# The weights of a spectral mix in halves through the ring of x, and loads moved across a stage boundary

## The chip, the cores and the metric

The kernel runs on one core of a Trainium2 chip. The metric is the device time of one execution in microseconds (us). Three timed runs of the kernel before gave a median of 3059.18 us (3055.52 to 3066.23). The profile is of one further execution, which took 3042.76 us; its span, from the first instruction to the last, is 3041.0 us.

The engines are PE (matrix products; PEld is its weight load), DVE and ACT (element-wise work; both can read PE's result memory, PSUM), POOL (element-wise work without PSUM, and DMAs), and SP (DMAs only). DMAs are issued on three queues, those of SP, ACT and POOL, and run on the same 16 DMA engines. Every queue, like every engine, takes its instructions in program order.

## The reference

The input x is (8, 32, 256, 256): 8 images, 32 channels, 256 x 256. Four layers follow each other; each normalises x over groups of two channels (zero mean, unit variance), applies a convolution of some kind and adds the result to x. The change lies in the first layer and in its seam with the second.

```
out_lo = einsum('bixy,ioxy->boxy', rfft2(gn(x))[:, :, :32, :32], w1)      # layer 0: 32 x 32 low modes,
out_hi = einsum('bixy,ioxy->boxy', rfft2(gn(x))[:, :, -32:, :32], w2)     # complex weights per mode
x = x + irfft2(zeros with out_lo, out_hi in their places) + bias
x = x + conv5x5(gn(x))                                                    # layer 1: one 5 x 5 kernel for all
x = x + gru_over_columns(gn(x))                                           # layer 2: recurrence along w
x = x + W @ [x, four running maxima of x] + b                             # layer 3
```

## The kernel before

**Forward transform and mix** (`forward_and_mix`). The forward transform goes over 64 units (`units`, eight images b by eight groups n of four channels). A unit's x is one tile `xa` of 1 MB (8 KB in each of 128 partitions), loaded by SP (L116) into a ring of AHEAD = 7 buffers: six loads are issued ahead, and then, ahead of unit u's work, that of unit u + 6. `over_columns(u)` (L118) multiplies by the constants `fw` (32 matmul records), squares x on ACT and on DVE (L140, L141) for the variance, and turns the result on DVE (L144) into `y`; its PSUM tile `yp` has three buffers. `over_rows(b, i)` (L148), four slices for an image, uses the constants `fh` and stands, for image b - 1, between the units 0 to 3 of image b. `turn`, `statistics` and `normalise` of image b - 1 come at the units 4, 5 and 7; `normalise` (L198) scales on DVE (L201), writes one half of the spectrum `xf` on ACT (L202) and the other, with real and imaginary parts swapped, by four POOL DMAs (L206).

The order is written out by hand (`manual_schedule(engines=None)`): each engine gets its instructions as the program lists them.

The mix (L252 on) has eight sets q of four kx; a set takes 256 recorded matmuls of 64 x 64 by 32, 128 for each half of ky. The weights of a set, `wt`, are 2 MB. Set 0 has a pool of its own, `mw`, and is loaded at unit (7, 2) (L217); sets 1 to 7 use a pool `mw2` of five buffers (L247) that is opened after the forward transform's pools are closed, so that its first loads wait for these. Results are copied from PSUM by ACT and DVE into `sm` (two buffers for each of two signs) and stored to the DRAM scratch `smd` on ACT's and SP's queue (L287).

**Inverse transform and 5 x 5 convolution** (`inverse_and_conv`). It goes over 16 units of 16 channels. `load_spectrum(b)` (L348) reads image b's spectrum from `smd` in three DMAs: one of 64 rows of 8 KB (L351) and two that pick 128 bytes at a time (L353), for images 0 and 1 on SP, later on ACT. `load(u, i)` (L383) reads a third of a unit's x, `xb`, in two POOL DMAs of 768 KB. Ahead of the loop stand the spectra of images 0 and 1, the x of unit 0, the sign turn of a half of spectrum 0 on DVE (L358), then `spectrum` (L369), a chain of small DVE instructions on the mean, and the inverse transform's matmuls (L410, L427).

**Around them.** `load_consts` (L39) issues eleven small loads on SP, and L107 that of `fh` (1 MB), ahead of x. `recurrence_weights` (L687) loads 384 KB `weights` and two small biases on POOL's queue and adds the biases on DVE (L698, L699), which waits for both; it is called ahead of everything else (L1089). `recurrence` and `maxima_and_mix`, some 2,000 us of the span, are not touched.

Of the kernel before, what the change touches and what calls it, by code (L numbers as in the profile page):

```python
# [9 lines left out]
F32 = mybir.dt.float32  # L10
# [6 lines left out]
P = 128  # L17
B, C, H, W = 8, 32, 256, 256
NG = 16
KM = 32  # L20
# [4 lines left out]
Q = H // A  # L25
# [13 lines left out]
def load_consts(tc, pool, d):  # L39
    nc = tc.nc  # L40
    k = Consts()
    for name in ("sign", "sel", "msel", "fw", "gw", "eh", "ident", "ident32", "pair", "valid", "conv"):
        t = pool.tile(list(d[name].shape), F32, name=f"c_{name}")
        nc.sync.dma_start(out=t, in_=d[name])
        setattr(k, name, t)
    k.mean = pool.tile([P, P], F32, name="c_mean")
    nc.vector.memset(k.mean, 1.0 / (2 * H * W))
    k.dc = pool.tile([P, P], F32, name="c_dc")
    nc.vector.memset(k.dc, 0.0)
    nc.vector.memset(k.dc[0:1], 1.0 / (H * W))  # L50
    k.ones = pool.tile([P, P], F32, name="c_ones")
    nc.vector.memset(k.ones, 1.0)
    k.mhalf = pool.tile([P, NG], F32, name="c_mhalf")
    nc.vector.memset(k.mhalf, -0.5)
    return k
# [18 lines left out]

def forward_and_mix(tc, k, d, smd, xmean):

# [7 lines left out]
    KC = 4  # L84
    AHEAD = 7
    SLICES = 4
    HW = float(H * W)
    with ExitStack() as ctx:
        one = ctx.enter_context(tc.tile_pool(name="m1", bufs=1))
        wp = ctx.enter_context(tc.tile_pool(name="mw", bufs=1))  # L90

# [3 lines left out]

        def load_weights(q, wp):
            wts[q] = wp.tile([P, KM, KC, C], F32, name=f"wt_{q}", tag="wt")
            nc.sync.dma_start(out=wts[q].rearrange("p y j o -> p (y j o)"), in_=d["wm"][q])

        with ExitStack() as inner:  # L100
            fwd = inner.enter_context(tc.tile_pool(name="a1c", bufs=1))
            xp = inner.enter_context(tc.tile_pool(name="a1x", bufs=AHEAD))
            wk = inner.enter_context(tc.tile_pool(name="a1w", bufs=2))
            sm = inner.enter_context(tc.tile_pool(name="a1s", bufs=2))
            ps = inner.enter_context(tc.tile_pool(name="a1p", bufs=1, space=PSUM))
            fh = fwd.tile([P, 2, HB, P], F32, name="fh")
            nc.sync.dma_start(out=fh, in_=d["fh"])  # L107
            junk = [fwd.tile([P, 2, 2 * H], F32, name=f"junk_{i}") for i in range(2)]
# [89 lines left out]
            def normalise(b):  # L198
                xb, rs = turned.pop(b)
                xb = xb.rearrange("p y x -> p (y x)")  # L200
                nc.vector.tensor_scalar_mul(xb, xb, rs)  # L201
                nc.scalar.activation(xf[:, 0, b].rearrange("p y x -> p (y x)"), xb, AF.Copy, scale=k.sign)  # L202
                for s in range(2):
                    for ri in range(2):
                        r, r2 = 64 * s + 32 * ri, 64 * s + 32 * (1 - ri)
                        nc.gpsimd.dma_start(  # L206
                            out=xf[r : r + 32, 1, b].rearrange("p y x -> p (y x)"), in_=xb[r2 : r2 + 32]
                        )

            with tc.manual_schedule(engines=None):  # L210
                for u in range(AHEAD - 1):
                    load(u)
                for u, (b, n) in enumerate(units):
                    if u + AHEAD - 1 < len(units):
                        load(u + AHEAD - 1)
                    if b == B - 1 and n == 2:
                        load_weights(0, wp)  # L217
                    over_columns(u)
                    if b > 0:
                        if n < SLICES:  # L220
                            over_rows(b - 1, n)
                        elif n == SLICES:
                            turn(b - 1)
                        elif n == SLICES + 1:
                            statistics(b - 1)
                        elif n == SLICES + 3:
                            normalise(b - 1)
                    if b == B - 1 and n == NK - 2:
                        for i in range(SLICES):
                            over_rows(b, i, 0, NK // 2)  # L230
                for i in range(SLICES):
                    over_rows(B - 1, i, NK // 2, NK)
# [13 lines left out]

        wp2 = ctx.enter_context(tc.tile_pool(name="mw2", bufs=5))  # L247
        sp = ctx.enter_context(tc.tile_pool(name="ms", bufs=2))
        ps = ctx.enter_context(tc.tile_pool(name="mp", bufs=4, space=PSUM))
        NQ = KM // KC  # L250
        KY = KM // 2
        with tc.manual_schedule(engines=None):  # L252
            for q in range(1, 6):
                load_weights(q, wp2)
            for q in range(NQ):
                if 2 <= q < 4:
                    load_weights(q + 4, wp2)
                wt = wts.pop(q)
                mps = [
# [4 lines left out]

                for ky in range(KM):
                    for j in range(0, KC, 2):
                        for s in range(2):
                            r = slice(64 * s, 64 * s + 64)
                            nc.tensor.matmul(
                                mps[s][ky // KY][32 * j : 32 * j + 64, :, :, ky % KY],  # L270
                                lhsT=wt[r, ky, j : j + 2, :].rearrange("p j o -> p (j o)"),
                                rhs=xf[r, :, :, ky, KC * q + j : KC * q + j + 2].rearrange("p r b x -> p (r b) x"),
                                start=True,
                                stop=True,
                            )
                for s in range(2):
                    sm = sp.tile([P, B, 2, KM], F32, name=f"sm_{q}_{s}", tag=f"sm{s}")
                    for h in range(2):
# [10 lines left out]
                        in_=sm.rearrange("p b r y -> p b (r y)"),  # L289
                    )  # L290


# [3 lines left out]

def inverse_and_conv(tc, k, d, smd, xmean, x2d, stb, first):

# [15 lines left out]
    with ExitStack() as ctx:  # L314
        one = ctx.enter_context(tc.tile_pool(name="a2c", bufs=1))
        xp = ctx.enter_context(tc.tile_pool(name="a2x", bufs=1))
        wk = ctx.enter_context(tc.tile_pool(name="a2w", bufs=2))
        sm = ctx.enter_context(tc.tile_pool(name="a2s", bufs=3))
        ps = ctx.enter_context(tc.tile_pool(name="a2p", bufs=1, space=PSUM))

        bias = one.tile([P, C], F32, name="bias0")
        nc.sync.dma_start(out=bias, in_=d["b0"].partition_broadcast(P))
        junk = one.tile([P, 16, Q], F32, name="junk")
# [6 lines left out]
        units = [(b, h) for b in range(B) for h in range(C // (2 * CH))]  # L330
        xs, specs, state = {}, {}, {}

# [13 lines left out]
        def load_spectrum(b):  # L346

            t = xp.tile([P, C, 2, KM], F32, name=f"spec_{b}", tag="spec", bufs=2)  # L348
            queue = nc.scalar if b > 1 else nc.sync
            modes = smd[b].rearrange("s x o r y -> (s x) o r y")  # L350
            queue.dma_start(out=t[0:64], in_=modes)  # L351
            for ro in range(2):
                queue.dma_start(out=t[64:128, :, ro], in_=modes[:, :, 1 - ro])  # L353
            specs[b] = t

        def turn(b, engine):
            t = specs[b]
            engine.tensor_scalar_mul(t[64:128, :, 1], t[64:128, :, 1], -1.0)  # L358
# [24 lines left out]
        def load(u, i):  # L383
            b, h = units[u]
            lo, hi = PIECES[i]
            for ch in range(2):
                t = xp.tile([P, hi - lo, CH, Q], F32, name=f"xb_{u}_{ch}_{i}", tag=f"xb{ch}{i}")
                nc.gpsimd.dma_start(
                    out=t.rearrange("p t c q -> p (t c q)"), in_=d["xl"][b, 2 * h + ch, :, lo * CH * Q : hi * CH * Q]
                )  # L390
                for p in range(lo, hi):
                    xs[u, ch, p] = t[:, p - lo]

# [215 lines left out]
        with tc.manual_schedule(engines=None):  # L609
            load_spectrum(0)  # L610
            load_spectrum(1)
            for i in range(3):
                load(0, i)
            turn(0, nc.vector)
            spectrum(0, means(0))
# [466 lines left out]
def kernel(ctx: ExitStack, tc: tile.TileContext, d: dict, out: bass.AP):  # L1082
# [5 lines left out]
    mv3 = pool.tile([P, B, 2], F32, name="mv3")  # L1088
    loaded = recurrence_weights(tc, pool, d)  # L1089
    smd = dram.tile([B, 2, KM, C, 2, KM], F32, name="smd")  # L1090
    x2d = dram.tile([B, W, A, C, Q], F32, name="x2d")
    x3d = dram.tile([W // 8, P, A, 2, 8 * Q], F32, name="x3d")
    fwd = dram.tile([W // 8, P, A, 2, 8 * Q], F32, name="fwd")
    forward_and_mix(tc, k, d, smd, xmean)
    with tc.tile_pool(name="later", bufs=1) as later:
        stb = later.tile([P, 3, B, C], F32, name="stb")
        first = later.tile([P, B, 8, Q], F32, name="first")
        inverse_and_conv(tc, k, d, smd, xmean, x2d, stb, first)
        recurrence(tc, k, d, x2d, x3d, fwd, stb, first, loaded, mean1, mv3)
# [119 lines left out]
```

## Time and profile before

| | us |
|---|---|
| timed runs, median of 3 | 3059.18 |
| profiled execution | 3042.76 |
| its span | 3041.0 |
| first matmul (unit 0) at | 15.33 |
| unit 8's first matmul at | 35.44 |
| unit 63's last matmul ends at | 203.3 |
| mix, first and last matmul | 216.2 to 292.1 |
| last store to `smd` issued at | 293.93 |
| sign turn of spectrum 0 at | 318.50 |
| first matmul of the inverse transform at | 320.35 |
| first matmul of the 5 x 5 convolution at | 342.93 |

Over the whole span PE is busy 92%, DVE 85%, ACT 61% and POOL 29%. That average says little about the part that is changed, which takes the first eighth of the span: there, stage by stage, one looks for the thing that ends last. A row of the view by windows gives the busy time of each engine in a stretch, the clock that PE was granted (1.00 is full speed) and the share of the 16 DMA engines' time in which they were busy (a little over 1 is possible, as packets overlap). The chain of waits is followed back from the last instruction; a line gives start, length and what the time went to.

### The profile page before, as it was taken

The page shows a single profiled execution, that of the slowest core. Times are in us where ns is not written, and L with a number is a line of the kernel's source. Part 1 is how long each engine was busy: PE and PEld are TensorE (multiplying, and loading weights), DVE is VectorE, ACT ScalarE, POOL GpSimd, SP SyncE. Part 2 cuts the span into 40 slices and gives each one's busy share as a digit, 9 for nine tenths or more (in the row PEclk, how much of TensorE's full clock was granted, in tenths as well). Part 3 has the DMA queues.
Part 4 walks back from the last instruction along what each step waited for, and adds up shares of the span by engine and source line. Part 5 has one row for each costly group of instructions (what it writes and reads, how often), then busy time and mean ns, then how long its engine had stood idle before and what let it go on. Part 6 is the DMA issues. An engine that isn't in the chain of part 4 may idle for free.

```text
span 3041.0 us, 111672 instructions
## 1 busy us (share of the span) xinstructions
PE 2787.3 (92%) x47736; PEld 1644.8 (54%) x47736; DVE 2580.6 (85%) x5172; ACT 1868.2 (61%) x4482; POOL 874.4 (29%) x1253
## 2 busy tenths in 40 slices
PE   7986799999999799999999999999999488888887
PEld 4666344444445466666666666666666233333333
DVE  5753688888888699999999999999999799999997
ACT  3432477777677678888888888888887122222222
POOL 0110022211121355555555555555555200000000
PEclk9995899999999899999999999999999799999988
DMA  9977677877765566566666667656674688888885
GB/s 380 392 282 220 202 223 232 240 230 219 230 209 163 140 152 165 142 141 146 165 160 144 141 146 168 157 141 142 150 168 113 205 325 325 324 326 329 333 332 224
DMA packets 468193, 655.69 MB, mean 216 GB/s; under 512 B 328784, under 2 KB 329696, under 8 KB 441456
## 3 DMA queue, kind: packets, MB, share of 16 engines
q1 hardware_dynamic: 407528, 487.89, 55.1%
q0 software_dynamic: 16784, 84.11, 8.3%
q10 hardware_dynamic: 43384, 76.55, 7.0%
q8 instruction: 374, 6.13, 0.8%
q14 instruction: 123, 1.01, 0.1%
HBM read 371.63 MB, written 272.63 MB: 212 GB/s over the span
## 4 chain that ended last, share of the span: by engine, by line
PE 71%; DVE 20%; issue 4%; DMA 3%; ACT 1%; SPq 0%; POOL 0%; ACTq 0%; DVEq 0%; POOLq 0%
PE r L772 14%; PE z L772 13%; PE vp L498 13%; PE ni L772 7%; PE nh L772 6%; PE up L427 4%; DVE rv L1031 4%; PE yp L131 3%; DVE dq L1037 2%; DVE uq L1039 2%; DVE m L1045 2%; DVE m L1043 2%; DVE m L1041 2%; PE sp L158 2%; PE tp L410 2%
## 5 line engine op out<-in xcount | busy, mean ns | idle before, releaser
L780 PE MATMUL z<-hs,weights 64*64 64x256 f32 x4080 | 539.4, 382 | 0.0
L780 PE MATMUL r<-hs,weights 64*64 64x256 f32 x4080 | 525.4, 375 | 0.0
L780 PE MATMUL ni<-hs,weights 64*64 64x256 f32 x4080 | 524.9, 375 | 0.0
L862 POOL TENSOR_TENSOR xw<-xw,hs 128x256 f32<-128x256 f32 x496 | 339.9, 685 | 635.8 <-DVE hs L861 634.1
L1077 ACT ACTIVATE ot<-o,bres 128x512 f32<-128x512 f32 x256 | 154.9, 688 | 505.5 <-PE o L1062 490.1
L531 DVE SCALAR_TENSOR_TENSOR x<-vp,r,x 128x128 f32<-128x128 f32 (+2 forms) x640 | 350.6, 563 | 90.5 <-PE vp L498 78.2
L498 PE MATMUL vp<-x,c_conv 64*64 64x384 f32 (+5 forms) x4608 | 422.1, 490 | 2.4 <-DVE x L531 2.4
L854 ACT ACTIVATE n<-n,bih 128x256 f32<-128x256 f32 x510 | 259.2, 508 | 187.8 <-DVE n L853 187.8
L856 POOL TENSOR_TENSOR a<-zm,xn 128x256 f32<-128x256 f32 x510 | 372.3, 730 | 6.4 <-ACT zm L849 6.1
L1062 PE MATMUL o<-m,wsc 32*32 32x512 f32 x3072 | 230.5, 728 | 108.7 <-DVE m L1045 103.7
L772 PE MATMUL r<-hs,weights 64*64 64x256 f32 x2040 | 319.0, 389 | 5.1 <-DVE hs L861 4.2
L772 PE MATMUL z<-xn,weights 64*64 64x256 f32 x2040 | 305.3, 376 | 15.2 <-DMA xw<-x2d 15.2
L498 PEld LDWEIGHTS vp<-x,c_conv 64*64 64x64 f32 x4608 | 221.7, 132 | 172.6 <-issue 93.8
L772 PE MATMUL r<-xn,weights 64*64 64x256 f32 x2040 | 305.7, 377 | 0.8 <-ACT rs L847 0.8
L772 PE MATMUL nh<-xn,weights 64*64 64x256 f32 x2040 | 305.7, 376 | 0.0
L772 PE MATMUL z<-hs,weights 64*64 64x256 f32 x2040 | 305.2, 376 | 0.0
L772 PE MATMUL ni<-hs,weights 64*64 64x256 f32 x2040 | 305.2, 376 | 0.0
L752 ACT ACTIVATE xn<-xw,shift,turned 128x256 f32<-128x256 f32 x496 | 290.6, 586 | 0.0
L848 DVE SCALAR_TENSOR_TENSOR n<-nh,bhh,rs 128x256 f32<-128x256 f32 x510 | 246.3, 483 | 45.8 <-ACT rs L847 31.6
L780 PEld LDWEIGHTS ni<-hs,weights 64*64 64x64 f32 x4080 | 284.5, 133 | 0.3
L780 PEld LDWEIGHTS r<-hs,weights 64*64 64x64 f32 x4080 | 281.2, 131 | 0.2
L847 ACT ACTIVATE rs<-r,brz 128x256 f32<-128x256 f32 x510 | 241.3, 473 | 53.1 <-PE r L780 32.5
(166 smaller groups left out, 6245.0 us busy)
## 6 DMA issues: line engine op xcount, KB each, us to landing
xb<-in_xl_dram POOLq DMA_DIRECT2D x96, 768.0 KB, 7.5
xa<-in_xt_dram SPq DMA_DIRECT2D x64, 1024.0 KB
x<-x3d SPq DMA_DIRECT2D x32, 2048.0 KB
fw<-fwd SPq DMA_DIRECT2D x32, 2048.0 KB
out_dram<-ot ACTq DMA_DIRECT2D x64, 1024.0 KB
xw<-x2d SPq DMA_DIRECT2D x248, 256.0 KB
fwd<-fm SPq DMA_DIRECT2D x248, 256.0 KB
x3d<-xw SPq DMA_DIRECT2D x248, 256.0 KB
```

The costliest lines, as they stand in the source:

```text
L498: ins = nc.tensor.matmul(vps[bank][to, :, dst], lhsT=k.conv[r, P : P + 64] if kind == 2 else k.conv[r, o], rhs=pair_of(u, ch, g, lo, hi, s ...
L531: nc.vector.scalar_tensor_tensor(x, src[o], r1[rows, g : g + 1], x, ALU.mult, ALU.add, accum_out=s1[rows, 0, n, ch, g : g + 1])
L752: nc.scalar.activation(norms[bi][:, b, w], raws[bi][:, b, w], AF.Identity, bias=shift[:, b : b + 1], scale=sc[:, 1, b : b + 1])
L772: ins = nc.tensor.matmul(out[r], lhsT=weights[r, kind, gate, :], rhs=src[r], start=start, stop=stop)
L780: ins = nc.tensor.matmul(out[pairs[1 - i]], lhsT=weights[r, kind, gate, :], rhs=prev[r, :, q0 : q0 + Q], start=False, stop=stop,)
L847: rs = nc.scalar.activation(r, p["r"], AF.Sigmoid, bias=brz[:, 0:1])
L848: nc.vector.scalar_tensor_tensor(m, p["nh"], bhh[:, 2:3], r, ALU.add, ALU.mult)
L854: nc.scalar.activation(m, m, AF.Tanh, bias=bih[:, 2:3])
L856: product = nc.gpsimd.tensor_tensor(a, zm, cur, ALU.mult)
L862: nc.gpsimd.tensor_tensor(raw, raw, new, ALU.add)
L1062: nc.tensor.matmul(pts[b2][i][32 * j : 32 * j + 32].rearrange("p (w q) -> p w q", q=Q), lhsT=wsc[q, b2, t, :], rhs=src[j][q, b2], start=first,
L1077: nc.scalar.activation(ot[:, i], pts[b2][i], AF.Identity, bias=bres[:, b2, i : i + 1])
```

## The change

- The constants get their tiles at once, but only `fw` is loaded ahead of x. `fh`, `sign`, `sel` and `msel` follow the fourth x, the others and the bias of layer 0 follow the seventh.
- The ring of x has 8 buffers and outlives the forward transform. The weights of the mix are cut into sixteen halves of 1 MB, which go through that ring behind x: half i is issued where x's unit 64 + i would be, and in the mix half 8 + i after the matmuls of half i. The pools `mw` and `mw2` are gone.
- `recurrence_weights` is called ahead of unit 16's work, inside the hand-written order.
- For the last image the four `xf` DMAs go to SP, ACT, POOL and SP.
- Unit 0's x of the inverse transform and the spectra lie in a pool at the other end of the on-chip memory, opened ahead of the mix. Its six loads are issued on SP in set 4 of the mix. Several pools wait for the tiles whose place they take instead of for the whole pool (`reuse_waits="tile"`).
- The three DMAs of spectrum 0 go to SP, ACT and POOL. The sign turn of its half is one ACT instruction, ahead of `spectrum` in the program.

The diff, cut to its core:

```diff
@@ load_consts
-        t = pool.tile(list(d[name].shape), F32, name=f"c_{name}")
-        nc.sync.dma_start(out=t, in_=d[name])
-        setattr(k, name, t)
+        setattr(k, name, pool.tile(list(d[name].shape), F32, name=f"c_{name}"))
+    k.bias = pool.tile([P, C], F32, name="bias0")
+
+    def load(*names):
+        for name in names:
+            nc.sync.dma_start(out=getattr(k, name), in_=d[name])
...
@@ forward_and_mix
-    AHEAD = 7
+    AHEAD = 8
...
-        wp = ctx.enter_context(tc.tile_pool(name="mw", bufs=1))
+        xp = ctx.enter_context(tc.tile_pool(name="a1x", bufs=AHEAD))
...
+        def load_weights(i):
+            if i < 2 * NQ:
+                q, h = divmod(i, 2)
+                wts[i] = xp.tile([P, KY, KC, C], F32, name=f"wt_{q}_{h}", tag="xa")
+                size = KY * KC * C
+                nc.sync.dma_start(
+                    out=wts[i].rearrange("p y j o -> p (y j o)"), in_=d["wm"][q, :, h * size : (h + 1) * size]
+                )
...
-                        nc.gpsimd.dma_start(
+                        queue = (nc.sync, nc.scalar, nc.gpsimd, nc.sync)[2 * s + ri] if b == B - 1 else nc.gpsimd
+                        queue.dma_start(
...
+                k.load("fw")
                 for u in range(AHEAD - 1):
                     load(u)
+                    if u == 3:
+                        nc.sync.dma_start(out=fh, in_=d["fh"])
+                        k.load("sign", "sel", "msel")
+                k.load("gw", "eh", "ident", "ident32", "pair", "valid", "conv")
+                nc.sync.dma_start(out=k.bias, in_=d["b0"].partition_broadcast(P))
                 for u, (b, n) in enumerate(units):
+                    if u == 16:
+                        more()
                     if u + AHEAD - 1 < len(units):
                         load(u + AHEAD - 1)
-                    if b == B - 1 and n == 2:
-                        load_weights(0, wp)
+                    else:
+                        load_weights(u + AHEAD - 1 - len(units))
...
+                load_weights(AHEAD - 1)
                 for i in range(SLICES):
                     over_rows(B - 1, i, NK // 2, NK)
...
-        wp2 = ctx.enter_context(tc.tile_pool(name="mw2", bufs=5))
-        sp = ctx.enter_context(tc.tile_pool(name="ms", bufs=2))
+        xp2 = keep.enter_context(tc.tile_pool(name="a2x", bufs=1, side="right", reuse_waits="tile"))
+        xb = conv_x(nc, d, xp2)
+        sp = ctx.enter_context(tc.tile_pool(name="ms", bufs=2, reuse_waits="tile"))
...
-            for q in range(1, 6):
-                load_weights(q, wp2)
             for q in range(NQ):
-                if 2 <= q < 4:
-                    load_weights(q + 4, wp2)
-                wt = wts.pop(q)
...
+                for h in range(2):
+                    wt = wts.pop(2 * q + h)
+                    for y in range(KY):
...
+                    load_weights(AHEAD + 2 * q + h)
+                if AHEAD + 2 * q in (2 * NQ, 2 * NQ + 1):
+                    for i in range(3):
+                        xb(0, 0, 0, i, nc.sync)
...
@@ conv_x: new, holds what load(u, i) of inverse_and_conv did, with the queue as an argument
...
@@ inverse_and_conv
-        one = ctx.enter_context(tc.tile_pool(name="a2c", bufs=1))
-        xp = ctx.enter_context(tc.tile_pool(name="a2x", bufs=1))
+        one = ctx.enter_context(tc.tile_pool(name="a2c", bufs=1, reuse_waits="tile"))
...
-            queue = nc.scalar if b > 1 else nc.sync
+            queues = (nc.sync, nc.scalar, nc.gpsimd) if b == 0 else 3 * (nc.scalar if b > 1 else nc.sync,)
...
             load_spectrum(0)
             load_spectrum(1)
-            for i in range(3):
-                load(0, i)
-            turn(0, nc.vector)
+            half = specs[0][64:128, :, 1]
+            nc.scalar.activation(half, half, AF.Copy, scale=-1.0)
             spectrum(0, means(0))
...
@@ tile_fno_conv_gru_directional_kernel
-    loaded = recurrence_weights(tc, pool, d)
+    loaded = []
+    keep = ExitStack()
...
-    forward_and_mix(tc, k, d, smd, xmean)
+    xp, xb = forward_and_mix(tc, k, d, smd, xmean, keep, lambda: loaded.extend(recurrence_weights(tc, pool, d)))
```

## The prediction, as it stood before the changed kernel ran

> **What bounds the kernel now.** I read the page's slices first: only the first five of 40 (380 us) hold code that the diff touches, and 2,700 us behind them keep their program. I asked the busy time by stage there; the cuts are at the first matmul, at unit 8's, at the end of unit 63's, at the mix's first and last, and at the first of the inverse transform.
>
> ```profile
> 0.00:15.30 15.30, 0.00 (x0) 0.00 (x1) 0.99 (x8) 1.37 (x2) 2.03 (x7) 1.00 0.78 258
> 15.30:35.40 20.10, 17.66 (x256) 9.93 (x256) 14.36 (x24) 9.14 (x17) 0.00 (x0) 1.00 1.01 427
> 35.40:204.00 168.60, 164.59 (x2844) 105.13 (x2844) 118.20 (x232) 70.60 (x118) 22.36 (x31) 1.00 0.96 372
> 204.00:216.20 12.20, 5.20 (x134) 4.70 (x135) 4.07 (x13) 2.30 (x2) 4.53 (x9) 0.84 0.33 83
> 216.20:292.20 76.00, 57.87 (x2048) 55.83 (x2048) 25.24 (x61) 21.87 (x61) 0.00 (x0) 0.52 0.73 246
> 292.20:320.40 28.20, 0.66 (x4) 0.56 (x4) 3.38 (x11) 1.36 (x4) 3.31 (x8) 0.50 0.93 248
> 320.40:349.60 29.20, 26.83 (x290) 10.21 (x291) 17.63 (x38) 17.05 (x52) 4.21 (x7) 0.92 0.55 176
> ```
>
> Columns: window, length, busy us (count) of PE, PEld, DVE, ACT, POOL, then PE clock, DMA share, GB/s. Four facts: PE stands still for 15.3 us at first; from 35.4 to 204 it is the bound (164.59 of 168.60 us); the mix takes 76.0 us for 57.87 of matmul; then PE waits 28.2 us. The chain of waits names what ended last:
>
> ```profile
> 6.70 8.49 DMA xa<-in_xt_dram
> ...
> 214.32 2.84 DMA xf<-xb
> ...
> 217.41 8.19 DMA wt<-in_wm_dram
> ...
> 293.93 3.51 DMA smd<-sm
> ```
>
> **1. Start: +3.0 us (1.5 to 4.5).** That x0 lands at 15.2 instead of about 6 is not the gain: units 0 to 7 go at the pace of the transfers (share 1.01), and PE becomes the bound at unit 8, whose x8 lands at 35.4. Ahead of x8 lie, before and after, x0 to x8, `fh` and all constants, in another order. What goes: from 2.0 to 10.2 us the queues were busy 63.2% (SP) and 18.7% (POOL), so idle 18% of 8.2 = 1.5 us while SP issued 12 small DMAs, and the 384 KB of `gru` took 1.5. Sum 3.0. Low end: the idle stays. High end: the constants' queue time (5.2 us less 1.4 for the 0.58 MB of `fh` in that window: 3.8) shrinks to that of 0.95 MB at 427 GB/s, 2.2. An eighth ring buffer is worth nothing where PE is the bound.
>
> **2. The recurrence's weights, moved to unit 16: -6.5 us (0 to -9.7).** This is the step that costs. It issues three POOL DMAs and two DVE instructions; the first of these (L698) waits for `bhh`. Ahead of them POOL has the four `xf` DMAs of image 0, and behind L698 on DVE stand the squares and the transpose of unit 16 and all after. At that place before:
>
> ```profile
> 60.59 0.70 DVE L201 TENSOR_SCALAR xb<-xb,rs 128x1024 f32<-128x1024 f32 x1
> ...
> 61.58 2.00 POOL L206 DMA_DIRECT2D xf<-xb  x4 [2.87 <-DVE xb L201]
> ...
> 70.25 1.93 PE L131 MATMUL yp<-xa,c_fw 128*32 128x256 f32 x32
> ```
>
> POOL ends `xf` at 63.58; three issues of 0.73, 0.56 and 0.55 (rows at 1.30 to 2.57) end at 65.4. The landing: 4.3 us at the start, and for `xf`, on the same queue beside x:
>
> ```profile
> DMA to landing us min/median/max: 2.2/7.9/10.1
> ```
>
> I take the median, the state being the same: 73.3. DVE, free at 61.3, stands 12 us; then squares 1.2 and transpose 0.7 give unit 16's PSUM buffer back at 75.2. There are three, so unit 19, at 70.25 above, starts 4.95 late, and nothing gives a PE-bound stage that back. A late clock comes on top: when PE ran dry at 208.0 its clock fell at about 212.3 (row 211 to 213: 0.83), and from 217.3 it needed until about 222.5 to return. Idle 4.9 reaches that 4.3; of 2.5 us at most I take 1.5. Ends: landing in 2.2 hides all; landing in 10.1 costs 7.2 + 2.5. x itself doesn't run short, since transfers go on meanwhile.
> The Trainium skill, TensorE: Matmul & The Clock Gate, section "HAM oscillation — how this bites in real kernels", speaks against it: idle gaps over some 3.4 us bring half the clock. By it the 2.5 would be certain, and this part -7.5.
>
> **3. Last `xf` on three queues: +1.2 us (0.6 to 1.6).** Four POOL issues take 1.99; the last, issued at 214.32, lands 2.84 later. On SP, ACT and POOL side by side the last is issued at 213.1 (behind ACT's copy: 213.7). The last unit's half of the weights stands ahead on SP; it waits for unit 63 (203.3) and is long through.
>
> **4. The mix: +9.3 us (-4.5 to +15.3).** Eight halves lie in the ring when it starts: the queue idles between 197 and 217, and PE's release of units 56 to 63 (177.7 to 203.3) issues them. So the wait for the second set, 223.6 to 225.64, goes. The rest is a pace. PE stops after every 127 to 128 matmuls and as many weight loads, and the instruction queue moved 374 packets for 95,472 PE instructions, 255 each:
>
> ```profile
> q8 instruction: 374, 6.13, 0.8%
> ```
>
> I read the stops as waits for code. Three such blocks, by their DMA share (last column but one):
>
> ```profile
> 232.78:239.01 6.23, 3.63 (x127) 3.50 (x127) 1.68 (x4) 1.45 (x4) 0.00 (x0) 0.50 1.02 424
> ...
> 244.99:249.05 4.06, 3.64 (x127) 3.50 (x127) 0.00 (x0) 0.71 (x2) 0.00 (x0) 0.50 0.67 159
> ...
> 285.03:288.84 3.81, 3.63 (x127) 3.49 (x127) 1.39 (x5) 1.17 (x4) 0.00 (x0) 0.50 0.64 126
> ```
>
> Saturated queues: 5.4 to 6.2 us a block, six times; else 3.6 to 4.1. After the change a half of the weights (1 MB, 2.43 us by the landings of x1 to x4) follows each of the first eight blocks: share about 0.65 plus the stores, in rows of 8 KB where 16 KB ran. Blocks 1 and 2 as before 6.4 together; seven at 4.4; two beside the 4.7 MB of first x (11 us, 6 KB rows) at 4.7; five at 3.8: 6.4 + 30.8 + 9.4 + 19.0 = 65.6 against 74.9 (217.2, where the last `xf` was in, to 292.1). Low end: the nine at 6.0, 79.4. High end: all fourteen at 3.8, 59.6. I sit nearer the 4.06 row, whose load is likest. SP's stores queue behind the first x; its PSUM and `sm` buffers give two sets of slack.
>
> **5. The spectra: +8.5 us (4.8 to 12.8).** The last `smd` lands at 297.4; the halves of spectrum 0 land at 316.6 and 318.5. Beside them ran six `xb` loads (4.7 MB, 299 to about 314); these now lie in the mix. What stays: from 314.5 to 322, almost alone, 5,109 packets of 128 bytes and 64 of 8 KB passed, so (7.5 - 1.2) x 16 / 5,109 = 20 ns a packet and engine. Spectrum 0 has 4,096, so 5.1 us, with 1.2 for its 8 KB rows and 2 to land: 8.3. But spectrum 1 no longer stands behind them on SP (its issue took 13.09 there); it runs beside ACT's and POOL's: 6,144 x 20 ns / 16 = 7.7, plus 2.4 and 2: 12.1, so 309.5. POOL's issue of 2,048 pieces is a microsecond or so longer (1,024 for `first` took 0.88). 318.5 - 309.5 = 9; I take 8.5. Ends: alone in 8.3 (12.8); all 8,192 pieces of both spectra first, at 23 ns (the large rows not set apart), 11.9 + 2.4 + 2 = 16.3 (4.8).
> The Trainium skill, DMA: Bandwidth & Descriptors, section "Issuing engines are not separate DMA queues", says that several issuers save issue time alone. By it the queues bring only SP's 4.09 us of issue less 1 or so, 3, and the rest is `xb`'s absence.
>
> **6. Small.** Sign turn on ACT: 0.6 for 1.15 (L202's whole tile) against DVE's 0.69, but beside DVE's chain (319.2 to 320.3) instead of ahead of it: +0.3 (0 to 0.7). Bias load and pools that wait by tile: nothing, as the data waits above end later.
>
> **Sum:** 3.0 - 6.5 + 1.2 + 9.3 + 8.5 + 0.3 = 15.8. Profiled: 3042.8 (span 3041.0, 1.8 around it) becomes 3027. The timed runs stand 16 us above that one (median 3059.2), with no stage to put it to, so I carry the difference: 3059.2 - 15.8 = **3043**. About 0.3%, 9.2 us, is what a measurement here tells from no change.
>
> **Rivals.**
> A, 62%: as summed, gain 9 to 25.
> B, 15%: `bhh` lands early and code comes at 3.8 a block: 15.8 + 6.5 + 6.0 = 28, 3031. For it: the start's 4.3 us landing; against: the median of 7.9.
> C, 10%: code is as slow beside halves as beside whole sets: 15.8 - 13.8 = 2, 3057. For it: blocks at share 0.92 took 5.76; against: the 4.06.
> D, 6%: first x isn't early, its pool waiting after all, so it stays beside the spectra: 15.8 - 8.5 = 7, 3052.
> E, 7%, slower: the stall at unit 19 leaves PE at half clock. Price: half of every us at 0.50; it decides beyond (15.8 + 9.2) x 2 = 50 us of it; to unit 63 there are 130, a loss of 65 and 3108. For it: from 226 to 324 the clock stayed 0.50 though PE was 95% busy from 266 on; against: twice it came back in 5 us.
>
> So faster 77%, within 0.3% 16% (C and D), slower 7%. Range: low is B less the 3.7 us by which the runs before went under their median, 3027; high is C and 3 of the 7 us by which they went over it, 3060. E is left out, and the outer parts of B and C.
>
> **What would show it.** Start: unit 8 at 32.4. Step 2: one DVE wait of about 12 us for `bhh`, PE idle 5 before unit 19. Mix: its first matmul near 219.5 (217.2 - 3.0 + 6.5 - 1.2), blocks near 4.4, `xb` in it. Spectra: 12 us from the last `smd` to the sign turn. Wrong if PE isn't the bound from unit 8, or the code isn't what stops the mix.

## The result, and the profile after

The changed kernel took 3055.39 us beside 3062.17 for the kernel before (medians of 20 runs each); the ratio is 0.9984, its interval 0.9971 to 0.9997. Timed once more (e14), it came out on the other side: 3056.33 beside 3051.16, ratio 1.0011 (0.9995 to 1.0027). One interval ends just below 1, the other reaches to either side: within 0.3%, and the forecast gain of 16 us didn't come.

As single profiled executions differ, there are three of each kernel. Their stages (means, us):

| stage | before | after | gain | predicted |
|---|---|---|---|---|
| start to unit 8's first matmul | 36.1 | 35.9 | +0.2 | +3.0 |
| unit 8 to the end of unit 63 | 168.4 | 179.1 | -10.7 | -6.5 |
| to the landing of the last `xf` | 13.9 | 12.9 | +1.0 | +1.2 |
| mix | 75.4 | 77.9 | -2.5 | +9.3 |
| end of the mix to the inverse transform | 28.2 | 19.1 | +9.1 | +8.8 |
| to the convolution's first matmul | 22.5 | 22.9 | -0.4 | 0 |
| sum: the convolution starts at | 344.5 | 347.8 | -3.3 | +15.8 |
| behind it, program unchanged | 2704.2 | 2706.0 | -1.8 | 0 |

The mix is counted from the landing of the last `xf`, as the chain of waits has it. Its loss of 2.5 is not clear of its own variation: the three of before are 75.0, 77.7 and 73.7, those of after 80.0, 78.6 and 75.1. With the eight variants below whose mix is the same (e1, e2, e6, e7, e8, e10, e11, e13) there are eleven profiles of it, from 73.7 to 80.0, mean 76.2. What is certain is that the forecast 9.3 didn't come. The first windows of the changed kernel's first profile, cut at the same events as those of before (columns as there):

```profile
0.00:6.20 6.20, 0.00 (x0) 0.03 (x1) 0.71 (x6) 1.40 (x2) 0.20 (x4) 1.00 0.69 237
6.20:36.20 30.00, 20.03 (x257) 11.14 (x261) 13.93 (x23) 9.32 (x17) 0.00 (x0) 0.83 0.95 367
36.20:214.90 178.70, 166.92 (x2848) 105.92 (x2840) 118.00 (x232) 70.38 (x118) 24.16 (x34) 0.97 0.99 376
214.90:228.00 13.10, 5.24 (x136) 4.75 (x136) 4.72 (x13) 2.30 (x2) 3.09 (x6) 0.85 0.71 223
228.00:307.90 79.90, 56.34 (x2048) 54.35 (x2048) 25.21 (x60) 21.96 (x61) 0.00 (x0) 0.54 0.69 213
307.90:327.60 19.70, 0.61 (x2) 0.51 (x3) 2.71 (x10) 2.35 (x5) 1.28 (x3) 0.50 0.93 134
```

The first row is 9 us shorter, the second 10 longer: PE starts early and then waits for x. In the third row PE is no longer busy all the time (166.9 of 178.7). The mix still takes 80 us for 56 of matmul. Of the others only the last row, the seam, is shorter. The chain of waits names what ended last:

```profile
2.60 10.93 DMA xa<-in_xt_dram
13.54 12.71 DMA c_gw<-in_gw_dram
26.27 6.50 DMA xa<-in_xt_dram
...
65.71 11.76 DMA bhh<-in_bhh_dram
...
224.19 3.63 DMA xf<-xb
...
309.66 3.37 DMA smd<-sm
...
313.29 12.08 DMA spec<-smd
```

A 144 KB constant stands in it for 12.7 us, a bias of 1.5 KB for 11.8.

**The start.** SP's waits in the first 40 us (us in all, times, longest):

```profile
SPq L48 <- DMA xa<-in_xt_dram: 6.1, 3, 2.1
SPq L127 <- DMA xa<-in_xt_dram: 5.1, 3, 2.1
...
SPq L48 <- DMA fh<-in_fh_dram: 3.3, 1, 3.3
```

SP stands before it issues a load, until an earlier one has landed. Counted along the program it is always the eighth before: x4 is issued when x0 is in, `gw` when x3 is, x7 when `gw` is. So eight DMAs at most are on their way, and while seven small constants are among them, little of x is. How much of the start this explains, e2 tells.

**Unit 16.** The row of DVE's first instruction on the biases (start, duration, and in brackets the wait ahead of it), and below it what PE waited for from 60 to 90 us:

```profile
77.56 0.16 DVE L727 TENSOR_TENSOR brz<-bih,bhh 128x2 f32<-128x2 f32 x1 [15.39 <-DMA bhh<-in_bhh_dram]
```
```profile
PE yp L142 <- DVE y L155: 8.5, 1, 8.5
```

Behind that idle PE ran at half clock for some 4 us (last column but two), then at full clock again:

```profile
79.70:84.00 4.30, 4.27 (x40) 1.99 (x44) 4.30 (x7) 0.00 (x0) 0.00 (x0) 0.50 0.91 305
84.00:88.00 4.00, 4.00 (x76) 2.68 (x72) 2.36 (x6) 0.00 (x0) 0.00 (x0) 0.97 0.94 315
```

This is the forecast's step 2 as it was described, only larger.

**The mix.** Three blocks of 128 matmuls, beside a half of the weights, between two halves, and beside the first x:

```profile
246.60:252.60 6.00, 3.63 (x127) 3.50 (x127) 2.18 (x6) 1.69 (x5) 0.00 (x0) 0.50 1.01 306
252.60:256.70 4.10, 3.63 (x129) 3.50 (x129) 0.96 (x3) 1.01 (x3) 0.00 (x0) 0.50 0.53 185
273.90:281.80 7.90, 3.63 (x127) 3.50 (x127) 1.68 (x4) 1.46 (x4) 0.00 (x0) 0.50 0.72 245
```

The matmuls take the same 3.63 in each; what differs is the stop at the end. A 1 MB half doesn't raise a block's share of DMA time evenly to 0.65, as the prediction had it: it comes as a burst at the block's head, which is where the next 16 KB of code are fetched. In the trace that packet starts 3.5 to 4.2 us after the block's first matmul beside a half, 1.6 to 2.4 between two, and up to 5.5 beside the first x; in the kernel before 3.1 to 4.0 beside whole sets and 1.0 where none was on its way. And PE goes on when it is in: over all 18 profiles PE stops in the mix for more than 1 us 133 times, and in 132 of them it goes on 1.1 to 1.7 us after the end of a packet of code. The one exception is the wait for the second set in the kernel before, at 225.6.

### The profile page after: what moved, and what is told of

It reads as the page before. It is cut to its first block, busy times and chain, and to the rows that moved or that the text cites. A ratio compares the mean times of both kernels' runs of the same rounds, so it can differ in the third digit from the quotient of the medians.

```text
span 3060.4 us, 111698 instructions
## 1 busy us (share of the span) xinstructions
PE 2791.9 (91%) x47736; PEld 1646.2 (54%) x47736; DVE 2579.4 (84%) x5171; ACT 1870.8 (61%) x4483; POOL 871.9 (28%) x1245
## 3 DMA queue, kind: packets, MB, share of 16 engines
q14 instruction: 123, 1.01, 0.1%
## 4 chain that ended last, share of the span: by engine, by line
PE 69%; DVE 20%; DMA 5%; issue 4%; ACT 1%; SPq 0%; POOL 0%; ACTq 0%; DVEq 0%; POOLq 0%
PE r L801 14%; PE z L801 13%; PE vp L528 11%; PE ni L801 7%; PE nh L801 6%; DVE rv L1060 4%; PE up L457 4%; PE yp L142 3%; DVE dq L1066 2%; DVE uq L1068 2%; DVE m L1074 2%; DVE m L1072 2%; DVE m L1070 2%; PE mp L286 2%; PE tp L440 2%
## 5 line engine op out<-in xcount | busy, mean ns | idle before, releaser
L528 PE MATMUL vp<-x,c_conv 64*64 64x384 f32 (+5 forms) x4608 | 425.8, 491 | 10.1 <-DVE x L561 10.1
```

Of the source, the lines that this page charges most:

```text
L528: ins = nc.tensor.matmul(vps[bank][to, :, dst], lhsT=k.conv[r, P : P + 64] if kind == 2 else k.conv[r, o], rhs=pair_of(u, ch, g, lo, hi, s ...
```

## The experiments

Each is an edit of the changed kernel, unless it says otherwise. Ratios are to the kernel before, timed beside it. Those of the six variants e1, e6, e7, e8, e11 and e12 lie between 0.9973 and 0.9988 with intervals that overlap, so the times don't rank them; what an edit does is read from the marks in its profile, one for each variant. First the four that take one suspected cost away.

**e1.** `recurrence_weights` ahead of everything, as in the kernel before:

```diff
-    loaded = []
+    loaded = recurrence_weights(tc, pool, d)
...
-    ... keep, lambda: loaded.extend(recurrence_weights(tc, pool, d)))
+    ... keep, lambda: None)
```

> The changed kernel, but the recurrence's weights and biases are loaded and added ahead of everything, as before the change. Theory: the DVE wait for the biases at unit 16 (15.4 us in the changed kernel's trace) emptied PE for 8.5 us and cost 2 more at half clock, and a PE-bound stage never gives that back. Then unit 63's last matmul ends at about 204 instead of 214.9, every later mark up to the convolution is 10.9 us earlier, and the time is 3055 - 11 = 3044. Rival: the stage is bound by x's transfers there, so that PE only waited a little earlier for what would have come late anyway; then unit 63 ends at 211 or later and the time falls by less than 4 us.

Unit 63 ended at 204.9, 10.0 earlier than in the profile of the changed kernel. Timed 3045.31 beside 3055.32 for the kernel before, 0.9977 (0.9959 to 0.9995). The stall's price in the forward transform is confirmed, and the rival, that x would have come late anyway, falls. But the mix began only 5.8 earlier: of ten won, four were lost ahead of the mix (e8 says to what).

**e2.** The small constants and the bias on POOL's queue instead of SP's.

```diff
-            nc.sync.dma_start(out=getattr(k, name), in_=d[name])
+            (nc.sync if name == "fw" else nc.gpsimd).dma_start(out=getattr(k, name), in_=d[name])
...
-                nc.sync.dma_start(out=k.bias, in_=d["b0"].partition_broadcast(P))
+                nc.gpsimd.dma_start(out=k.bias, in_=d["b0"].partition_broadcast(P))
```

> The changed kernel, but all small constants except the first product's go over POOL's queue instead of SP's; the same bytes, the same place in the program. Theory: SP had no more than about eight DMAs unlanded at a time, so the eleven small ones between the big ones kept x4 to x8 from being issued (x7 went out at 26.3 us, with the queues idle around 20 and 30 us). With them off SP, x stays in flight without a break and unit 8's first matmul comes at 31 to 33 us instead of 36.0; marks behind unit 16 move by the same 3 to 5 us. Rival: the constants cost their own transfer time wherever they are; then unit 8 stays at 35 to 36.

```profile
0.00:6.20 6.20, 0.00 (x0) 0.00 (x0) 0.60 (x5) 1.28 (x1) 4.68 (x12) 1.00 0.58 186
6.20:35.20 29.00, 19.24 (x256) 10.02 (x257) 14.38 (x24) 9.23 (x17) 1.61 (x3) 0.88 1.01 404
```

Unit 8 started at 35.2, 0.6 before the mean of the changed kernel: the rival held. SP no longer waits for a constant, but up to unit 8 the DMA engines are busy for 32.9 us (6.2 at 0.58, 29 at 1.01), as in the changed kernel (32.8). So the queue isn't the point, and SP's waits are the smaller part (e7, without the small loads, wins 5.2): ahead of x8 the small loads take on POOL the time that they take on SP.

**e3.** Halves 8 to 15 of the weights aren't loaded; those sets use halves 0 to 7 again, so that the output isn't the reference's.

> The changed kernel, but the halves 8 to 15 of the mix's weights are not loaded: sets 4 to 7 multiply by the weights of sets 0 to 3, so 8 MB of loads are left out and the output is another. The first x is still loaded in set 4. Theory: PE's code comes in packets of 16 KB that wait behind whatever the queues hold, so blocks of 127 matmuls come at 3.8 us as soon as the loads beside them go; the eight blocks of sets 0 to 3 then take about 30 us instead of 41, blocks beside the first x stay at 5 to 8, and the mix takes 66 to 70 instead of 79.9. Rival: the pace is PE's own at half clock, with its waits for buffers; then the mix stays within 3 us of 79.9.

```profile
228.70:294.40 65.70, 54.38 (x2046) 52.50 (x2046) 25.22 (x60) 21.92 (x61) 0.00 (x0) 0.55 0.45 132
```

The row begins with the third matmul. From the landing of the last `xf` the mix took 66.2 instead of 77.9 on the mean, its blocks 3.4 to 4.3, and 7.1 and 6.3 only beside the first x. By the mean of three eight halves cost 11.7 us, by that of eleven 10.0: 1.2 to 1.5 each, though their 2.4 us of transfer lie fully beside matmuls and PE never waits for the weights themselves. The rival, a pace of PE's own at half clock, falls: the clock is as low here (0.55). What the stop waits for isn't named by a semaphore; that it is code rests on its place (every 255 instructions, 128 matmuls), on the code packets, whose end it follows 132 times of 133, and on this run.

**e4.** The first x back behind the mix, on POOL behind the spectra.

```diff
-                if AHEAD + 2 * q in (2 * NQ, 2 * NQ + 1):
-                    for i in range(3):
-                        xb(0, 0, 0, i, nc.sync)
...
             load_spectrum(1)
+            for i in range(3):
+                load(0, i)
```

> The changed kernel, but the first unit's x is loaded on POOL's queue behind the spectra, as before the change, instead of in set 4 of the mix. Theory: it took its 11 us of transfer from the mix, where PE's code waits for it, and gave them to the spectra; without it, blocks 8 to 15 of the mix come at 3.8 us, so the mix is 10 us shorter (70), and the spectra take 19 to 21 us from the last store instead of 12: the first matmul of the convolution moves by less than 3 us. Rival, as I predicted: the mix hides the first x; then the mix is no more than 2 us shorter and the convolution begins 6 to 8 us later.

The mix took 72.7, less than any of the eleven (5.2 below the mean of three, 3.6 below that of eleven), the seam 30.2 (11.0 above it). So moving the first x forward wins 11 in the seam and pays 4 to 5 in the mix; the truth lies between the two expectations. The prediction charged the mix 1.8 for it (two blocks at 4.7 instead of 3.8).

**e5, e9, e14, e15.** Both kernels unchanged, for the table above.

> The kernel before, unchanged, profiled once more: its first profile (3042.8 us) was shorter than every later timed run of it (3050 to 3071). In the first profile the convolution's first matmul stood at 342.9 us and its matmuls ran until 992.8, 649.9 us later; in the changed kernel and its variants that stretch took 655 to 668. Theory, the stretch of the convolution varies from run to run with the stores that DVE waits for, and the start does not: convolution begins at 342 to 345 and runs 655 to 668. Rival, the start varies: convolution begins at 350 or later and runs 650.

> The changed kernel, unchanged, profiled once more, as its timed median (3055.4 us) and its profiled run (3062.2) stand 7 apart. The start up to unit 16 and the mix should repeat within 1.5 us. Theory, the landing behind which DVE stands at unit 16 varies with the state of the queues (8 to 12 us), so PE's idle before unit 19 is 5 to 8.5 and the convolution starts between 346 and 351; the stretch behind it, as in the other runs, takes 2698 to 2717 whatever the change. Rival, both repeat to within 1 us and the 7 lie behind the convolution's start.

> The changed kernel, unchanged, timed beside the kernel before once more. Theory, its start part repeats (unit 19 at 79.8, convolution at 348 to 351) and the stretch behind it takes 2698 to 2720, so that the two kernels' medians lie within 6 us of each other, the changed one between 2 slower and 5 faster. Rival, the changed kernel is really 5 to 7 faster for a reason behind the convolution's start: the median again 5 or more below, and the stretch in its profile under 2700.

> The kernel before, unchanged. Convolution at 343 to 347 if its start repeats as in two profiles, the stretch behind it 2698 to 2715. If the kernel before has starts of 350 and more as well, they are what the timed difference comes from.

The kernel before: convolution at 342.9, 346.6 and 343.9, the stretch behind 2698.0, 2706.6 and 2708.1. The changed one: 350.8, 348.3 and 344.4, and 2709.7, 2706.4 and 2702.0. The stall repeats (unit 19 at 79.7, 79.8, 79.4); e9's theory that its landing varies falls. In e14 the convolution began earlier than expected (344.4, not 348 to 351), and the median was 5 above the kernel before, not at most 2. The mix varies (80.0, 78.6, 75.1), and the unchanged stretch does, over all profiles from 2695.7 to 2719.9. The profile on which the prediction stood had a short one, 8.6 to 10.1 below the other two, which is over half of the 16 us between it and the timed median. The gain of the first timing didn't return in e14, so its rival, a reason behind the convolution's start, falls too. The two chains of waits through the convolution that stand furthest apart, of e13 and of e11 (shares by line):

```profile
by line: PE vp L528 61.0%; PE up L457 20.6%; PE tp L440 8.8%; PE v L490 3.3%; PE s L600 2.3%; ACT junk L483 1.5%; DVE x L561 0.9%; issue 0.6%; ACT junk L568 0.5%; PE s L402 0.3%; DVE x L466 0.2%; ACTq L568 0.0%
```
```profile
by line: PE vp L533 51.9%; PE up L462 16.3%; PE tp L445 7.2%; DMA spec<-smd 6.1%; DMA x2d<-x 4.9%; PE v L495 2.5%; DVE x L566 2.2%; PE s L605 1.9%; issue 1.6%; ACT junk L488 1.4%; SPq L592 0.9%; SPq L591 0.9%; ACT junk L573 0.7%; SPq L587 0
```

In the long one 11% of the chain are stores of the convolution and the spectra they queue with; in the short one there are none. Why one execution runs into them and another doesn't is open.

**e6.** The two DVE instructions alone at unit 48; the three loads stay at unit 16.

```diff
                     if u == 16:
                         more()
+                    if u == 48:
+                        biases()
...
```

`biases` holds the two instructions, taken out of `recurrence_weights`.

> The changed kernel with the two DVE instructions on the recurrence's biases moved from unit 16 to unit 48; the three loads stay at unit 16. Theory, all of that step's loss is DVE standing in order behind a landing: no DVE wait, no idle of PE before unit 19, unit 63 ends near 204 instead of 214.9, and the timed median falls by 10 us below that of the changed kernel (to 3045), as in the variant that loads them first. Rival, the 0.39 MB beside a saturated stream of x cost something themselves, because x then comes late: unit 63 ends at 208 or later.

Unit 63 ended at 204.3 and DVE didn't wait. Timed 3046.55 beside 3053.83, 0.9973 (0.9958 to 0.9988). The whole loss of step 2 is the place of one small DVE instruction; the transfers beside x cost nothing that shows.

**e7.** The eight small constants behind the last half of the weights.

```diff
-                k.load("gw", "eh", "ident", "ident32", "pair", "valid", "conv")
-                nc.sync.dma_start(out=k.bias, in_=d["b0"].partition_broadcast(P))
...
                 load_weights(AHEAD - 1)
+                k.load("gw", "eh", "ident", "ident32", "pair", "valid", "conv")
+                nc.sync.dma_start(out=k.bias, in_=d["b0"].partition_broadcast(P))
```

> The changed kernel with gw, eh, ident, ident32, pair, valid, conv and the bias (0.82 MB in eight loads) issued behind the last half of the weights instead of ahead of x7. Theory, these loads cost about 6 us of the transfers wherever they stand ahead of x8: x0 lands at 6.1, eight more loads of 2.45 us and fh of 2.45 follow, with 0.3 for the three that stay, so unit 8 starts at 28.5 to 30 instead of 36.2 and unit 63 ends 6 to 7 earlier, at 208 to 209. Rival, only their bytes count (0.82 MB at 427 GB/s): unit 8 at 34, 2 us earlier. Second rival, PE at its lower clock is the bound there: unit 8 at 33 to 36.

Unit 8 started at 30.6, 5.2 us earlier, and unit 63 ended at 209.4, 5.6 earlier: near the theory's 6 and far from the 2.0 of their bytes (0.87 MB at 427 GB/s). Timed 3047.75, 0.9986 (0.9969 to 1.0003).

**e8.** Both together.

> Both together, biases added at unit 48 and the eight constants behind the weights. If the two losses are separate they add up: unit 63 ends at 198 to 199 (16 before 214.9), the mix starts at 212, the convolution at 334 to 335, and the timed median lies 16 us below that of the changed kernel, near 3039, some 20 under the kernel before. If the ring of x is again short at unit 16, when the weights join, half of the second gain is lost: unit 63 at 202.

Unit 63 ended at 198.5, as expected, but the last `xf` was in only at 220.1, 21.6 us later instead of 12.9. SP's waits there, and the chain:

```profile
SPq L48 <- DMA wt<-in_wm_dram: 11.5, 4, 4.7
```
```profile
199.68 17.13 DMA c_eh<-in_eh_dram
...
216.83 3.30 DMA xf<-xb
```

`xf` stands behind constants that wait for halves still on their way, the eighth before again, counted over SP and ACT together. The DMA share was 1.01 to 1.02 from 180 to 210: with PE's stall gone, the 8 MB of halves are what is late next. Timed 3046.07, 0.9977 (0.9959 to 0.9994), so of the 16 at unit 63 ten were kept at the convolution's start (338.0, where 334 to 335 was expected).

**e11.** Biases at unit 48, and the eight constants one by one behind the units 20 to 34:

```diff
-                k.load("gw", "eh", "ident", "ident32", "pair", "valid", "conv")
-                nc.sync.dma_start(out=k.bias, in_=d["b0"].partition_broadcast(P))
+                later = ("gw", "eh", "ident", "ident32", "pair", "valid", "conv")
...
                     over_columns(u)
+                    if u % 2 == 0 and 20 <= u < 34:
+                        k.load(later[(u - 20) // 2])
+                    if u == 34:
+                        nc.sync.dma_start(out=k.bias, in_=d["b0"].partition_broadcast(P))
```

> Biases added at unit 48, and the eight constants issued one by one behind the units 20 to 34, where PE is the bound and x runs seven units ahead. In the variant with both late, unit 63 ended at 198.5 but the mix began only at 220.6, as the last xf stood on SP behind the constants and behind halves of the weights still in flight (DMA share 1.01 to 1.02 until 210). Theory, the constants cost nothing here, and only the halves are still ahead of xf: unit 8 at 30.5, unit 63 at 198.5, the mix from 214 to 217, the convolution from 332 to 335, the timed median 16 to 19 below that of the changed kernel's profile-based 3059 or about 13 below the kernel before, near 3041. Rival, the transfers are the bound of the whole forward part once PE no longer stops, wherever the constants lie: mix again at 219 to 221, convolution at 337 to 339.

Unit 63 ended at 200.5, 2 us later than in e8, and the last `xf` was in only at 219.7, 9.9 us after its issue. The mix began at 219.9 and the convolution at 336.9: the rival held in the main, and what delays `xf` is not the constants. That it is the halves, e12 shows. Timed 3046.96, 0.9988 (0.9974 to 1.0002).

**e12.** As e11, and the halves 5 to 7 issued behind the last `xf`.

```diff
-                        load_weights(u + AHEAD - 1 - len(units))
+                        if u + AHEAD - 1 - len(units) < 5:
+                            load_weights(u + AHEAD - 1 - len(units))
...
-                load_weights(AHEAD - 1)
...
                 normalise(B - 1)
+                for i in range(5, AHEAD):
+                    load_weights(i)
```

> As the variant with constants spread, and the halves 5 to 7 of the weights issued on SP behind the last xf instead of ahead of it. If halves in flight delay xf, it now lands 3.6 after its issue, and the mix starts at 212 to 213; but the three halves then fall into the first blocks of the mix, whose code waits behind them: 2 to 2.5 each for three blocks, 6 in all, so the mix lasts 80 to 82. Theory: conv starts within 2 of the spread variant, 331 to 336. Rival, the mix doesn't pay, as one burst holds up one or two blocks at most: convolution at 329 to 331, timed near 3037.

The last `xf` was in at 213.7, 3.6 us after its issue, the mix took 79.9 and the convolution began at 334.2: the theory. The mix was 5 us longer than in e11, but 79.9 lies within the spread of 73.7 to 80.0, so one profile doesn't show that the halves cost it this. Timed 3045.61, 0.9983 (0.9968 to 0.9999).

**e10.** The three DMAs of spectrum 0 back on SP.

```diff
-            queues = (nc.sync, nc.scalar, nc.gpsimd) if b == 0 else 3 * (nc.scalar if b > 1 else nc.sync,)
+            queues = 3 * (nc.scalar if b > 1 else nc.sync,)
```

> The changed kernel with the three DMAs of spectrum 0 back on SP; the first x stays in the mix. It divides the 8.5 us by which the seam became shorter. Theory, the pieces of 128 bytes on the DMA engines set the time: spectrum 1 no longer runs beside spectrum 0 but behind it, SP's issue (4.1 us for three, as in the kernel before) comes on top, and the halves land 12 to 14.5 us after the last store, so the three queues bring 0 to 2 and the absence of the first x all the rest; the seam is 20 to 22 instead of 19.75. Rival, the queues are most of it: the halves land 16 to 17 after the last store and the seam is 24 to 25.

Both sides were wrong: the seam became 15.7, 3.5 shorter than with three queues. In a timeline the sign turn shows when the second half was in (issue of the first DMA: 307.95):

```profile
317.21 1.05 ACT L643 ACTIVATE spec<-spec 64x1024 f32<-64x1024 f32 x1 [13.21 <-DMA spec<-smd]
```

That is 9.3 us after the issue, against 12.4, 11.6 and 11.4 in the three profiles of the changed kernel (there to the first matmul on the spectrum, which waits for the last half).

**e13.** Three queues for spectrum 0, but spectrum 1 on ACT behind the sign turn.

```diff
-            queues = (nc.sync, nc.scalar, nc.gpsimd) if b == 0 else 3 * (nc.scalar if b > 1 else nc.sync,)
+            queues = (nc.sync, nc.scalar, nc.gpsimd) if b == 0 else 3 * (nc.scalar,)
...
-            load_spectrum(1)
             half = specs[0][64:128, :, 1]
             nc.scalar.activation(half, half, AF.Copy, scale=-1.0)
+            load_spectrum(1)
```

> The changed kernel with spectrum 0 still on SP, ACT and POOL, but spectrum 1 issued on ACT behind the sign turn, so that nothing runs beside spectrum 0. Theory, it is spectrum 1's 4,096 small pieces beside those of spectrum 0 that cost the changed kernel 3 to 4 us: the halves now land 8 to 9.5 us after the issue (11.4 to 12.4 before) and the seam is 15 to 16.5. Rival, the three queues as such are slower than SP alone (POOL's issue 1.13, ACT behind its store): the halves land 11 or more after the issue and the seam stays at 18.5 to 20. Spectrum 1 lands some 10 us later than before, at 330 or so; the first use of it comes behind the convolution's start.

```profile
309.43 7.54 DMA spec<-smd
```

The seam was 14.7, the last half in 8.2 us after the first issue (308.8 to 317.0). So spectrum 1 beside spectrum 0 is what costs 3 to 4 us. Three queues with nothing beside (8.2) against one (9.3 in e10, 8.4 in e16) are worth at most 1 us.

The Trainium skill, DMA: Bandwidth & Descriptors, section "Issuing engines are not separate DMA queues", says that several issuers save issue time alone; that at most a microsecond is won here agrees.

**e16.** What the runs singled out: biases at unit 48, constants spread, halves 5 to 7 behind `xf`, spectrum 0 on SP.

> Biases at unit 48, constants spread over units 20 to 34, halves 5 to 7 behind the last xf, and spectrum 0 on SP. The convolution started at 334.2 without the last; with a seam shorter by 3 to 4 it should start at 330 to 331.5, 16 to 20 before the changed kernel and 12 to 16 before the kernel before. With 2698 to 2717 behind it and 1.8 around, the time is 3030 to 3050, the median 9 to 13 below that of the kernel before. Rival, the stretch behind the start gives part of it back: the median 7 below, as in the other variants.

```profile
6.30:30.50 24.20, 17.90 (x256) 10.06 (x257) 14.27 (x24) 9.16 (x17) 0.00 (x0) 0.93 1.00 412
30.50:202.00 171.50, 165.82 (x2844) 106.32 (x2844) 118.14 (x232) 70.59 (x118) 24.16 (x34) 1.00 1.02 384
...
215.50:293.60 78.10, 58.47 (x2046) 56.42 (x2046) 25.22 (x60) 21.88 (x61) 0.14 (x2) 0.50 0.80 255
293.60:308.50 14.90, 0.65 (x5) 0.55 (x4) 2.71 (x10) 2.38 (x5) 0.00 (x0) 0.50 0.84 140
```

The convolution starts at 331.4, as expected, 13.1 before the mean of the kernel before. Timed 3039.36 beside 3051.16, 0.9967 (0.9950 to 0.9983), and the changed kernel's 3056.33 (e14): it beats both. The mix, at 78, is what the idea hasn't improved even here.

## Why the prediction was wrong

**Step 4, the mix, is the one that failed.** It stood at +9.3 and came out at -2.5 by three profiles each, and at -0.8 by all eleven. That the wait for the second set goes was right, and so was that code is what stops PE. That halves let code through faster was wrong: the term "seven at 4.4" came out at 38.1 us for 30.8 in the first profile, 5.4 a block. "I sit nearer the 4.06 row, whose load is likest" averaged a burst and the silence behind it into a share. Blocks ran 6.0 and 4.1 to 4.7 by turns, and 6.5 to 7.9 beside the first x, where two blocks at 4.7 had been put. The low end, -4.5, had the right pace beside data (6.0), though not for every block, and rival C, at 10%, came nearest for this step.

**Step 2** had the mechanism, the place and the order of events right. The landing was the term mis-sized: 11.8 instead of the median 7.9 of another tile's on that queue, so PE idled 8.5 instead of 4.95; the late clock cost 2.2 (from unit 19's first matmul to unit 24's 14.1 instead of 11.9), not 1.5. Sum 10.7, past the range's end of 9.7, for the row's longest landing, 10.1, wasn't a bound for a DMA of tiny rows behind 384 KB on the same queue.

**Step 1** was worth 0.2, not 3.0. The idle of the DMA engines up to unit 8 was 3.4 us before (15.3 at 0.78) and is 3.4 after (6.2 at 0.69, 30 at 0.95): it wasn't removed. Of it 1.9 still lie ahead of 6.2 us, and 1.5 behind, where SP stands for the eighth DMA before; e2, where SP doesn't, started unit 8 only 0.6 earlier. Nor did the 1.5 for `gru` come: with `gru` gone the DMA engines were busy as long (32.8 us after, 32.2 before). Why is open. That units 0 to 7 go at the transfers' pace, and that an early x0 is no gain, was right. What the constants cost in the changed kernel, 5.2 us (e7), stands ahead of x8 behind x6.

**Step 3**: 1.0 for 1.2, partly by luck. The last `xf` lands 3.6 after the first of the four issues, as the halves ahead of it were "long through"; that was so only with PE's stall. Without the stall it took 7.7 (e1), 6.9 (e6) and 9.9 (e11).

**Step 5** came out at 9.1 for 8.5 + 0.3, with the landings at 11.4 to 12.4 for 12.1. Of its parts, the absence of the first x is worth 11 (e4), and the three queues with spectrum 1 beside lose 3 to 4 (e10, e13). The prediction had both numbers, 8.3 alone (8.2 in e13) and 12.1 beside, and took the split for part of the gain, where the split was the loss.

**The baseline.** The sum was made against a profile 16 us under the timed median, and the difference carried. Three profiles show that the stretch behind the change varies by more than any term of the sum (24 us over all profiles); the stage sums, not the totals, are what such a change is to be judged by. Rival E didn't come: the clock returned behind unit 19 (mean 0.97 to unit 63).

## What to carry to other kernels

A constant or a bias costs by its place in the queues, not by its bytes: an engine's instruction on it goes where the load has long landed, and its load where nothing is paced by transfers. Where transfers and instruction fetch share the DMA engines, judge a stop by what is in the queue at the moment of the fetch, not by the mean share. And when a stall goes, ask what was late behind it: here part of each gain ahead of the mix went to halves still in flight.

## What the runs showed of the hardware

- Code for PE (374 packets of 16 KB) waits behind data: 1 MB put at a block's head costs PE 1.2 to 1.5 us on the mean (e3), and blocks beside such loads take 6.0 with rows of 8 KB as with 16 KB. The Trainium skill, Runtime: NRT & Kernel Launch, section "Instruction fetch mechanics", calls the cost of a crossing mostly hidden; for 128 matmuls of 28.6 ns (3.63 over 127) beside saturated queues it isn't.
- 0.87 MB in eight loads with short rows held up x by 5.2 us, 2.5 times their bytes at 427 GB/s (e7).
- A bias of 1.5 KB on POOL's queue, behind 384 KB and beside a saturated stream, landed 11.8 us after its issue; at the start of the kernel before, 4.3.
- In these programs a DMA on SP or ACT waits for the landing of the eighth before it on the two queues together (start, e8).
